# Rows sent to the experts without waiting for each other, and a later layer's keys and values made while they travel: a two-layer perceiver on one Trainium2 core

## The chip, the cores and the metric

The kernel runs on one core of a Trainium2 chip, all of it in float32. The metric is the device time of one execution in microseconds (us), lower is better. Engines are named as in the profile: PE is the matrix engine (TensorE) and PEld its weight loads, DVE the vector engine, ACT the scalar engine, POOL the GpSimd engine, SP the engine that issues most DMAs. "Cold" and "warm" stand for the half and the full TensorE clock that the profile's PEclk shows.

## The reference

A perceiver of two layers works on x of 16 × 64 rows of 256 (1024 rows in all) with a memory of 16 batches × 1601 rows. Each step adds to x what it makes of a layer norm of x:

```
x = x + L0_xattn(ln(x), memory)      # attention on the memory, 32 best scores of each row
x = x + L0_attn(ln(x))               # retention
x = x + L0_ffn(ln(x), ...)           # attention over 16 positions, then experts
x = x + L1_xattn(ln(x), memory)      # 16-head attention on the normed memory
x = x + L1_attn(ln(x))               # random features
x = x + L1_ffn(ln(x))                # fast feed-forward trees, then attention
```

The change lies in L0_ffn and in the start of L1_xattn:

```
y1 = _ln(x + _mha(x)) * ln1_g + ln1_b
# _moe: each row goes to its best of 8 experts, 128 rows for each expert
gates = softmax(y1 @ wg); idx = argmax(gates)
loc   = place of the row among those of the same expert
slot  = idx * cap + loc   if loc < cap else dropped
disp  = zeros.at[slot].set(y1)
h = disp @ w1 + b1 ;  y = h @ w2 + b2          # for each expert
out = gate_val * y[slot]                       # 0 for dropped rows
return _ln(y1 + out) * ln2_g + ln2_b
# L1_xattn, for each of the 16 batches:
qn, kn = layernorm(q), layernorm(memory)
Q, K, V = qn @ Wq + bq, kn @ Wk + bk, kn @ Wv + bv
```

## The kernel before, in words

All of x stands in the tile X, eight blocks of 128 rows (NB = 8, HALVES are blocks 0 to 3 and 4 to 7). A framework orders the instructions of each engine from the program's order, its data dependences, and the buffers of its pools; only the units of layer 1's attention (L1101 on) have an order written out by hand. A tile with a tag is one of a few buffers of its pool, so a new one waits until an older one is read.

The stages around the change:

- **Early memory.** Layer 1 needs for each of the 16 memory batches: the load (`load_mem`, L215 to L218, 1.6 MB into `memt`, two buffers), its normalisation (`normalise`, statistics on DVE at L415, the rows scaled on POOL at L426), its transposes (`turned_mem`, 26 transposes "pt" at L439 in eight groups, each copied by ACT at L444 into `mT`), its keys (`keys`, 8 tiles "ps_k" of two matmuls at L460, copied by ACT into kT at L468) and its values (`values`, 8 tiles "ps_v" at L482, copied into v at L490 or by ACT). For the first batches, 0 and 1, this is called early: fetches of 0 and 1, transposes, keys and values of batch 0, the fetch of batch 2, and the transposes of batch 1. In the program's text it stands behind L0_ffn, but the scheduler moves its instructions up into L0_ffn wherever PE would wait. Its PSUM pool `ps_early` has two buffers. A float32 matmul shows as two records, each a "pass" here.
- **MHA.** The transposes of xa = ln(X) (L165, "ps_t" in `transposed`), the projections of queries and keys ("ps_p", L183) and of values ("ps_n", L197), then four groups of two softmaxes: scores "ps_h" (L664), their mask and softmax on DVE (L672 to L684, the exponential on ACT), transposes "pt" (L688), "po" (L697), whose copies make oT; the output projection ("ps_n" again, L197), and `scaled`, which makes y1 by halves: moments on DVE (L141, L142), a square root on ACT (L144), its reciprocal (L145), and two DVE operations for each block.
- **Routing.** y1 is transposed, "ps_g" (L780) makes the gates, DVE picks the expert, "ps_c" (L810, L812) counts places, DVE makes `to_row` and `from_row`.
- **Scatter.** Eight indirect DMAs on POOL (L842) write the rows of y1 to the DRAM tensor `disp`, and one DMA on SP (L846) reads all of it into `dsp`:

```
for k in range(NB):
    nc.gpsimd.indirect_dma_start(out=disp, out_offset=...(ap=to_row[:, k : k + 1], axis=0),
        in_=y1[:, k, :], in_offset=None)
nc.sync.dma_start(out=dsp, in_=disp[0:NT, :].rearrange("(e p) d -> p e d", p=P))
```

  The framework sees eight writes to one tensor, at rows that it doesn't know.
- **Experts.** `dsp` is transposed (dT, L165), and for each of 8 experts "ps_h" (L859) and "ps_y" (L873, L876) follow, the copy `ye` on ACT (L878), and its store to `done`. The weights of an expert, 2 MB, come on SP through two buffers.
- **Gather.** Eight indirect DMAs on POOL (L883) fetch `back`, DVE adds each to y1 (L887), and when all are in the program, `scaled` norms y1 by halves into xa (L721) and `joined` (L892) adds each block to X.
- **Layer 1 begins.** qn is a norm of X (`layernorm`, L154 on DVE), transposed (L165) and copied by ACT (L944) into qnT, then projected: "ps_p" (L183), "ps_n" (L197). Then come the units.

At L1281 near the kernel's end, tree node scores are made with small matmuls, much as at L780.

Of the kernel before, what the change touches and what calls it, by code (L numbers as in the profile page):

```python
# [9 lines left out]
F32 = mybir.dt.float32  # L10
I32 = mybir.dt.int32
# [5 lines left out]
P = 128  # L17
# [48 lines left out]
def perceiver_kernel(  # L66
# [80 lines left out]

    HALVES = ((0, 4), (4, 4))

    def layernorm(dst, src, scale=1.0, bias=eps):  # L150
        for k0, n in HALVES:
            mv, rstd = moments(src, k0, n, scale, bias)
            for k in range(n):
                nc.vector.tensor_scalar(  # L154
                    dst[:, k0 + k, :], src[:, k0 + k, :], mv[:, k, 0:1], rstd[:, k : k + 1],
                    ALU.subtract, ALU.mult,
                )

    def transposed(src, pool, write):

        for half in range(2):
            for c in range(2):
                ps = pool.tile([P, 512], F32, name="ps_t", tag="mm")
                for j in range(4):
                    nc.tensor.transpose(  # L165
                        ps[:, j * P : (j + 1) * P],
                        src[:, half * 4 + j, c * P : (c + 1) * P],
                        ident,
                    )
                write(c, half, ps)  # L170
# [261 lines left out]
    def turned_mem(mt, mT, pool):  # L432

        for part, dc in TURN_STEPS:
# [12 lines left out]
            )  # L447
            yield

    def new_mT():  # L450
        return kvp.tile([P, 2, S], F32, name="mT", tag="mT")

    def keys(mT, kT, pool):

        for part, oc in KEY_STEPS:
            c0, _, n = PARTS[part]
            n0 = c0 * P
            ps = pool.tile([P, 512], F32, name="ps_k", tag="mm")
            for dc in range(2):
                nc.tensor.matmul(  # L460
                    ps[:, 0:n],
                    lhsT=wk[:, dc, oc * P : (oc + 1) * P],
                    rhs=mT[:, dc, n0 : n0 + n],
                    start=(dc == 0),
                    stop=(dc == 1),
                )
            yield
            nc.scalar.activation(  # L468
                kT[:, oc, n0 : n0 + n], ps[:, 0:n], AF.Identity, bias=col("L1_bk", oc)
            )  # L470
            yield

    def values(mT, v, pool, copy):

        c0 = 0
        for n in VALUE_STEPS:
            m = chunk(c0)
            ps = pool.tile([P, 2, D], F32, name="ps_v", tag="mm")
            for j in range(n):
                c = c0 + j  # L480
                for dc in range(2):
                    nc.tensor.matmul(  # L482
                        ps[0 : chunk(c), j, :],
                        lhsT=mT[:, dc, c * P : c * P + chunk(c)],
                        rhs=wv[:, dc, :],
                        start=(dc == 0),
                        stop=(dc == 1),
                    )
            yield
            copy(v[0:m, c0 : c0 + n, :], ps[0:m, 0:n, :])  # L490
            c0 += n
            yield
# [17 lines left out]
            pass  # L510

    kvs_of[0] = x1.enter_context(tc.tile_pool(name="x1_kv0", bufs=1))


    with ExitStack() as ph:
# [75 lines left out]
    with ExitStack() as ph:  # L591
# [21 lines left out]
        xa = keep.tile([P, NB, D], F32, name="xa")  # L613
        layernorm(xa, X)
        y1 = keep.tile([P, NB, D], F32, name="y1")

        with ExitStack() as sub:
            act = sub.enter_context(tc.tile_pool(name="mha_act", bufs=1))
# [94 lines left out]

            project(ps_m, w[:, 3, :, :], oT, add_mha)

        def scaled(dst, src, g, then):

            for k0, n in HALVES:
                mv, rstd = moments(src, k0, n)
                for k in range(n):  # L720
                    nc.vector.scalar_tensor_tensor(  # L721
                        dst[:, k0 + k, :], src[:, k0 + k, :], mv[:, k, 0:1], row(g),
                        ALU.subtract, ALU.mult,
                    )
                    then(k0 + k, rstd[:, k : k + 1])
# [4 lines left out]
            )  # L730

        scaled(y1, xa, "ln1_g", shifted)

        nc.gpsimd.tensor_tensor(
            X, X, row("ln2_b").unsqueeze(1).to_broadcast([P, NB, D]), ALU.add
# [2 lines left out]
        with ExitStack() as sub:  # L738
# [55 lines left out]
            nc.vector.reduce_sum(out=gs, in_=gates, axis=AX.X)  # L794
            nc.vector.reciprocal(gs, gs)
            nc.vector.tensor_tensor(gates, gates, gs.unsqueeze(2).to_broadcast(wide), ALU.mult)
            gval = act.tile([P, NB], F32, name="gval")
            nc.vector.reduce_max(out=gval, in_=gates, axis=AX.X)
            ranks = rank.unsqueeze(1).to_broadcast(wide)
            cand = act.tile(wide, F32, name="cand")  # L800
# [8 lines left out]
            ps = ps_x.tile([P, NB, NE], F32, name="ps_c", tag="mm")  # L809
            nc.tensor.matmul(ps, lhsT=before, rhs=mask, start=True, stop=False)  # L810
            for k in range(1, NB):
                nc.tensor.matmul(  # L812
                    ps[:, k:NB, :],
                    lhsT=ones,
                    rhs=mask[:, k - 1 : k, :].to_broadcast([P, NB - k, NE]),
                    start=False,
                    stop=(k == NB - 1),
                )
# [13 lines left out]
            to_row = act.tile([P, NB], I32, name="to_row")  # L832
            nc.vector.tensor_copy(to_row, slot)
            nc.vector.tensor_scalar(slot, slot, float(NT - 1), None, ALU.min)
            from_row = act.tile([P, NB], I32, name="from_row")
            nc.vector.tensor_copy(from_row, slot)
            nc.vector.tensor_tensor(gval, gval, fits, ALU.mult)


            dsp = act.tile([P, NE, D], F32, name="dsp", tag="y1T")  # L840
            for k in range(NB):
                nc.gpsimd.indirect_dma_start(  # L842
                    out=disp, out_offset=bass.IndirectOffsetOnAxis(ap=to_row[:, k : k + 1], axis=0),
                    in_=y1[:, k, :], in_offset=None,
                )
            nc.sync.dma_start(out=dsp, in_=disp[0:NT, :].rearrange("(e p) d -> p e d", p=P))  # L846
            dT = act.tile([P, 2, NT], F32, name="dT")
            transposed(dsp, ps_x, to_cols(dT))

            b1_at = COLS["moe_b1"][0]  # L850
            for e in range(NE):
                w1, w2, b2 = experts.pop(e) if e in experts else load_expert(e)
                hT = work.tile([P, 8, CAP], F32, name="hT", tag="hT")
                for g in range(2):
                    ps = ps_x.tile([P, 4, CAP], F32, name="ps_h", tag="mm")
                    for j in range(4):
                        f0 = (g * 4 + j) * P
                        for dc in range(2):
                            nc.tensor.matmul(  # L859
                                ps[:, j, :],  # L860
                                lhsT=w1[:, dc, f0 : f0 + P],
                                rhs=dT[:, dc, e * CAP : (e + 1) * CAP],
                                start=(dc == 0),
                                stop=(dc == 1),
                            )
                    at = b1_at + e * 8 + g * 4
                    nc.vector.tensor_tensor(
                        hT[:, g * 4 : (g + 1) * 4, :], ps,
                        cols[:, at : at + 4].unsqueeze(2).to_broadcast([P, 4, CAP]), ALU.add,
                    )  # L870
                ps = ps_x.tile([P, D], F32, name="ps_y", tag="mm")
                for f in range(8):
                    nc.tensor.matmul(  # L873
                        ps, lhsT=hT[:, f, :], rhs=w2[:, f, :], start=(f == 0), stop=False
                    )
                nc.tensor.matmul(ps, lhsT=ones[0:1, :], rhs=b2, start=False, stop=True)  # L876
                ye = work.tile([P, D], F32, name="ye", tag="ye")
                nc.scalar.copy(ye, ps)  # L878
                nc.scalar.dma_start(out=done[e * CAP : (e + 1) * CAP, :], in_=ye)

            for k in range(NB):
                back = work.tile([P, D], F32, name="back", tag="back", bufs=4)
                nc.gpsimd.indirect_dma_start(  # L883
                    out=back, out_offset=None, in_=done,
                    in_offset=bass.IndirectOffsetOnAxis(ap=from_row[:, k : k + 1], axis=0),
                )
                nc.vector.scalar_tensor_tensor(  # L887
                    y1[:, k, :], back, gval[:, k : k + 1], y1[:, k, :], ALU.mult, ALU.add
                )

        def joined(k, rstd):
            nc.vector.scalar_tensor_tensor(  # L892
                X[:, k, :], xa[:, k, :], rstd, X[:, k, :], ALU.mult, ALU.add
            )

        scaled(xa, y1, "ln2_g", joined)


    for b in range(2):
        run(fetch(b))  # L900
    for b in range(2):
        mTs[b] = new_mT()
        run(turned_mem(mems.pop(b), mTs[b], ps_early))
        if b == 0:
            kvs[0] = new_kv(0)
            mT = mTs.pop(0)
            run(keys(mT, kvs[0][0], ps_early))
            run(values(mT, kvs[0][1], ps_early, nc.scalar.copy))
            run(fetch(2))
    early.close()  # L910

    with x1 as ph:
# [23 lines left out]


        qn = act.tile([P, NB, D], F32, name="qn", tag="b")
        layernorm(qn, X, 1.0 + EPS, eps2)
        qnT = act.tile([P, 2, NT], F32, name="qnT", tag="a")  # L940

        def normed(dst, wname, bname):
# [552 lines left out]
```

## Time and profile before

| | us |
|---|---|
| median of 3 runs | 1711.45 (1711.29 to 1711.51) |
| the profiled execution | 1709.81 |
| its span, first to last instruction | 1708.1 |
| PE busy in it | 1512.6 (89%) |
| DVE busy | 1021.2 (60%) |
| ACT busy | 814.6 (48%) |
| POOL busy | 212.0 (12%) |
| mean granted TensorE clock | 0.954 |

The times in the views are of this one execution. In the row of slices the span is cut into 40 equal parts and each digit is a busy share in tenths. A row of a windows table gives the stretch, then the busy time of each engine with the number of instructions, then the granted clock and what the DMA engines did. A row of the timeline gives the start, the busy time, engine, line, operation, output and inputs, and in brackets the idle time ahead of it with what ended it. A row of the chain of waits gives a start, a length, and the engine and operation that the end of the kernel was waiting for.

### The profile page before, as it was taken

To read this page: it belongs to the slowest core of one execution; us is meant where nothing else is said; L and a number is where in the kernel's file an instruction comes from. 1 tells how busy PE (TensorE), PEld (TensorE's weight loads), DVE (VectorE), ACT (ScalarE), POOL (GpSimd) and SP (SyncE) were. 2 spreads that over 40 slices of the span, in tenths; PEclk is the share of its full clock that TensorE was granted. 3 is DMA by queue.
4 is the path that set the end of the run, shared out by engine and by line. 5 is a ranking of instruction groups with operands and counts; after the bars stand their busy time and mean duration, and the time that the engine had idled before them with its cause. 6 is when DMAs were issued, how large, how long until landed. Compare 5 with 4: busy or idle time off the path is not lost.

```text
span 1708.1 us, 27877 instructions
## 1 busy us (share of the span) xinstructions
PE 1512.6 (89%) x10992; PEld 1008.2 (59%) x10992; DVE 1021.2 (60%) x2197; ACT 814.6 (48%) x1984; POOL 212.0 (12%) x405
## 2 busy tenths in 40 slices
PE   4899979992939999999999999999999973889997
PEld 3555546672836666666666666666667652544455
DVE  2667847771145777677767776777766665333122
ACT  3455531350005766666667666766666551212121
POOL 0000004201010120222021202120210001000000
PEclk9999989995969999999999999999999996889999
DMA  9044203223910101110011101110100003100000
GB/s 316 1 154 138 94 19 108 83 91 97 287 58 1 40 3 41 40 41 15 29 40 41 34 11 41 40 41 3 41 2 3 3 3 122 66 1 0 0 0 25
DMA packets 76034, 92.84 MB, mean 54 GB/s; under 512 B 2408, under 2 KB 71072, under 8 KB 75776
## 3 DMA queue, kind: packets, MB, share of 16 engines
q1 hardware_dynamic: 72064, 80.85, 14.9%
q0 software_dynamic: 2688, 9.17, 1.9%
q8 instruction: 86, 1.41, 0.4%
q10 hardware_dynamic: 1152, 1.05, 0.2%
q14 instruction: 44, 0.36, 0.1%
HBM read 85.82 MB, written 5.24 MB: 53 GB/s over the span
## 4 chain that ended last, share of the span: by engine, by line
PE 72%; ACT 10%; DVE 9%; issue 4%; DMA 3%; SPq 1%; POOL 0%; ACTq 0%; DVEq 0%; POOLq 0%
PE ps_v L482 10%; PE ps_k L460 7%; ACT a L997 6%; PE sc L981 6%; PE po L1029 6%; PE pt L1010 5%; PE ps_h L1334 5%; PE ps_p L183 3%; PE ps_o L1352 3%; PE pt L248 3%; PE sc L290 3%; PE pu L346 3%; PE pt L439 2%; PE ps_n L197 2%; DVE nmax L995 2%
## 5 line engine op out<-in xcount | busy, mean ns | idle before, releaser
L997 ACT ACTIVATE a<-sc,nmax 128x384 f32<-128x384 f32 (+2 forms) x512 | 300.3, 596 | 170.8 <-DVE nmax L995 170.5
L995 DVE TENSOR_REDUCE nmax<-sc 128x1 f32<-128x384 f32 (+2 forms) x512 | 258.2, 567 | 109.8 <-PE sc L981 109.7
L482 PE MATMUL ps_v<-w_x,mT 128*128 128x256 f32 (+1 forms) x832 | 205.3, 385 | 22.3 <-ACT kT L468 22.3
L1010 PEld LDWEIGHTS pt<-ident,a 128*128 128x128 f32 (+1 forms) x1664 | 189.3, 141 | 52.1 <-issue 28.2
L1017 DVE COPY aT<-pt 128x512 f32<-128x512 f32 (+1 forms) x288 | 191.0, 685 | 37.8 <-PE pt L1010 30.8
L1010 PE MATMUL pt<-ident,a 128*128 128x128 f32 (+1 forms) x1664 | 207.5, 274 | 2.3 <-ACT kT L468 0.7
L460 PE MATMUL ps_k<-mT,w_x 128*128 128x384 f32 (+2 forms) x512 | 207.9, 528 | 0.1
L482 PEld LDWEIGHTS ps_v<-w_x,mT 128*128 128x128 f32 (+1 forms) x832 | 144.7, 186 | 49.6 <-ACT kT L468 31.3
L460 PEld LDWEIGHTS ps_k<-mT,w_x 128*128 128x128 f32 x512 | 87.4, 190 | 108.1 <-issue 77.6
L1029 PE MATMUL po<-aT,v 128*32 128x128 f32 (+1 forms) x3328 | 119.1, 277 | 10.9 <-DVE aT L1017 7.0
L444 ACT ACTIVATE mT<-pt,cols 128x384 f32<-128x384 f32 (+2 forms) x128 | 87.1, 684 | 79.0 <-PE pt L439 76.3
L981 PE MATMUL sc<-kT,qh 32*128 32x384 f32 (+2 forms) x1024 | 123.1, 548 | 0.0
L426 POOL TENSOR_SCALAR memt<-memt,m_nmean,m_rstd 128x256 f32<-128x256 f32 (+1 forms) x208 | 112.2, 557 | 7.3 <-PE po L1029 4.3
L997 ACT ACTIVATION_READ_ACCUMULATOR a<-sc,nmax 128x1 f32 x512 | 105.1, 205 | 0.0
L1029 PEld LDWEIGHTS po<-aT,v 128*32 128x32 f32 (+1 forms) x3328 | 82.7, 109 | 35.5 <-issue 13.5
L490 DVE COPY v<-ps_v 128x512 f32<-128x512 f32 (+1 forms) x120 | 69.2, 576 | 49.3 <-PE po L1029 30.7
L415 DVE BATCH_NORM_STATS2 m_st<-memt 128x6 f32<-128x256 f32 (+1 forms) x208 | 82.6, 401 | 3.4 <-DMA memt<-in_mem_dram 3.0
L1334 PE MATMUL ps_h<-xnT,fw 128*128 128x512 f32 x192 | 84.1, 596 | 0.0
L253 ACT COPY mT<-pt 128x512 f32<-128x512 f32 (+1 forms) x128 | 58.0, 503 | 53.3 <-PE pt L248 52.6
L248 PE MATMUL pt<-ident,memt 128*128 128x128 f32 (+1 forms) x416 | 63.2, 292 | 22.8 <-DMA memt<-in_mem_dram 21.6
L468 ACT ACTIVATE kT<-ps_k,cols 128x384 f32<-128x384 f32 (+2 forms) x128 | 76.0, 593 | 13.2 <-PE ps_k L460 13.2
L1015 ACT COPY aT<-pt 128x512 f32<-128x512 f32 x128 | 76.9, 601 | 0.7 <-PE pt L1010 0.7
(310 smaller groups left out, 1945.8 us busy)
## 6 DMA issues: line engine op xcount, KB each, us to landing
memt<-in_mem_dram SPq DMA_DIRECT2D x32, 1536.0 KB, 9.1
w<-in_moe_w_dram SPq DMA_DIRECT2D x16, 1024.0 KB, 5.1
fw<-in_fff_w_dram SPq DMA_DIRECT2D x6, 1024.0 KB, 12.8
memt<-in_mem_dram SPq DMA_DIRECT2D x32, 65.0 KB
w_x<-in_w_x_dram POOLq DMA_DIRECT2D x2, 1024.0 KB, 12.2
rows<-in_rows_dram POOLq DMA_DIRECT2D x1, 1430.5 KB, 9.9
X<-in_x_dram SPq DMA_DIRECT2D x1, 1024.0 KB
w_mha<-in_w_mha_dram POOLq DMA_DIRECT2D x1, 1024.0 KB
```

The lines of the kernel that those rows point to most:

```text
L248: nc.tensor.transpose(pt[:, j * P : j * P + chunk(c)], mems[h][0 : chunk(c), c, dc * P : (dc + 1) * P], ident[0 : chunk(c), 0 : chunk(c)],)
L426: nc.gpsimd.tensor_scalar(mt[0:m, c, :], mt[0:m, c, :], nmean[0:m, c : c + 1], rstd[0:m, c : c + 1], ALU.add, ALU.mult,)
L444: nc.scalar.activation(mT[:, dc, c0 * P : c0 * P + n], pt[:, 0:n], AF.Identity, bias=col("L1_norm_b", dc), scale=col("L1_norm_w", dc),)
L460: nc.tensor.matmul(ps[:, 0:n], lhsT=wk[:, dc, oc * P : (oc + 1) * P], rhs=mT[:, dc, n0 : n0 + n], start=(dc == 0), stop=(dc == 1),)
L482: nc.tensor.matmul(ps[0 : chunk(c), j, :], lhsT=mT[:, dc, c * P : c * P + chunk(c)], rhs=wv[:, dc, :], start=(dc == 0), stop=(dc == 1),)
L981: nc.tensor.matmul(scs[j][:, 0:n], lhsT=qh[rs, oc, b, :, :], rhs=kT[rs, oc, c0 * P : c0 * P + n], start=True, stop=True,)
L995: nc.vector.reduce_max(out=nm, in_=sc[:, 0:n], axis=AX.X, negate=True)
L997: nc.scalar.activation(aj[:, 0:n], sc[:, 0:n], AF.Exp, bias=nm, accum_out=tot[:, blk, part : part + 1])
L1010: nc.tensor.transpose(pt[0:m, j * P : (j + 1) * P], a[j][:, c * P : c * P + m], ident)
L1017: nc.vector.tensor_copy(aT[0:m, :], pt[0:m, :])
L1029: nc.tensor.matmul(po[32 * j : 32 * j + 32, :], lhsT=v[0:m, c0 + c, blk * 32 : (blk + 1) * 32], rhs=aTs[c][0:m, j * P : (j + 1) * P], star ...
L1334: nc.tensor.matmul(ps, lhsT=fw1[:, f, dc, m * P : (m + 1) * P], rhs=xnT[:, dc, cs], start=(dc == 0), stop=(dc == 1),)
```

## The change

Scatters: the eight indirect writes are declared independent of each other, and the read of `disp` gets a dependence on each of the eight by hand. Gathers: each half is fetched, added, normed and joined to X before the second half is fetched in the program's text. Early memory: the transposes of batch 0 are called after y1; its keys are held behind the last "ps_c" matmul and dT's transposes behind its last key matmul; its values are held behind the last expert's last matmul; the transposes of batch 1 and the fetch of batch 2 are called after that. The norm qn is called by halves, the first at high priority, and in it every second block is made by ACT (Identity, with scale and a bias `ln_off` that DVE makes) instead of DVE. The tiles `gval` and `from_row` move to a pool that lives longer.

```diff
-    def layernorm(dst, src, scale=1.0, bias=eps):
-        for k0, n in HALVES:
+    def layernorm(dst, src, scale=1.0, bias=eps, halves=HALVES, shared=False):
+        for k0, n in halves:
             mv, rstd = moments(src, k0, n, scale, bias)
+            if shared:
+                off = small.tile([P, NB], F32, name="ln_off", tag="ln_off")
+                nc.vector.scalar_tensor_tensor(
+                    off[:, 0:n], mv[:, 0:n, 0], -1.0, rstd[:, 0:n], ALU.mult, ALU.mult
+                )
             for k in range(n):
+                if shared and k % 2:
+                    nc.scalar.activation(
+                        dst[:, k0 + k, :], src[:, k0 + k, :], AF.Identity,
+                        bias=off[:, k : k + 1], scale=rstd[:, k : k + 1],
+                    )
+                    continue
...
+    def early_memory(b):
+        run(fetch(b))
+        mTs[b] = new_mT()
+        run(turned_mem(mems.pop(b), mTs[b], ps_early))
...
         scaled(y1, xa, "ln1_g", shifted)
+        early_memory(0)
...
             dsp = act.tile([P, NE, D], F32, name="dsp", tag="y1T")
+            sent = []
             for k in range(NB):
-                nc.gpsimd.indirect_dma_start(
+                sent.append(nc.gpsimd.indirect_dma_start(
                     out=disp, out_offset=bass.IndirectOffsetOnAxis(ap=to_row[:, k : k + 1], axis=0),
                     in_=y1[:, k, :], in_offset=None,
-                )
-            nc.sync.dma_start(out=dsp, in_=disp[0:NT, :].rearrange("(e p) d -> p e d", p=P))
+                ).ins)
+                for other in sent[:-1]:
+                    tc.declare_no_dep(sent[-1], other, reason="rows of disp")
+            read = nc.sync.dma_start(
+                out=dsp, in_=disp[0:NT, :].rearrange("(e p) d -> p e d", p=P)
+            ).ins
+            for one in sent:
+                tc.add_manual_dep(
+                    read, one.name,
+                    mybir.DependencyInfo(mybir.DependencyClass.Sync, mybir.DependencyReason.DATA),
+                    reason="rows of disp",
+                )
+            mT0 = mTs[0]
+            kvs[0] = new_kv(0)
+            with tc.issue_after(counted.ins):
+                run(keys(mT0, kvs[0][0], ps_early))
             dT = act.tile([P, 2, NT], F32, name="dT")
-            transposed(dsp, ps_x, to_cols(dT))
+            with tc.issue_after(made[-1].ins):
+                transposed(dsp, ps_x, to_cols(dT))
...
+            with tc.issue_after(last.ins):
+                run(values(mTs.pop(0), kvs[0][1], ps_early, nc.scalar.copy))
+            def joined(k, rstd):
                 nc.vector.scalar_tensor_tensor(
-                    y1[:, k, :], back, gval[:, k : k + 1], y1[:, k, :], ALU.mult, ALU.add
-                )
...
+                    X[:, k, :], xa[:, k, :], rstd, X[:, k, :], ALU.mult, ALU.add
+                )
+            for half in HALVES:
+                for k in range(half[0], half[0] + half[1]):
+                    back = work.tile([P, D], F32, name="back", tag="back", bufs=4)
+                    nc.gpsimd.indirect_dma_start(
...
+                    nc.vector.scalar_tensor_tensor(
+                        y1[:, k, :], back, gval[:, k : k + 1], y1[:, k, :], ALU.mult, ALU.add
+                    )
+                scaled(xa, y1, "ln2_g", joined, (half,))
-    for b in range(2):
-        run(fetch(b))
-    for b in range(2):
-        mTs[b] = new_mT()
-        run(turned_mem(mems.pop(b), mTs[b], ps_early))
-        if b == 0:
-            kvs[0] = new_kv(0)
-            mT = mTs.pop(0)
-            run(keys(mT, kvs[0][0], ps_early))
-            run(values(mT, kvs[0][1], ps_early, nc.scalar.copy))
-            run(fetch(2))
+    early_memory(1)
+    run(fetch(2))
...
-        layernorm(qn, X, 1.0 + EPS, eps2)
+        with tc.high_priority():
+            layernorm(qn, X, 1.0 + EPS, eps2, HALVES[0:1], True)
+        layernorm(qn, X, 1.0 + EPS, eps2, HALVES[1:2], True)
```

What the change moves in the instruction order of each engine: on PE, batch 0's keys leave MHA for the place between "ps_c" and dT's transposes, its values leave MHA and the output projection for the place behind the last "ps_y", and batch 1's transposes follow them; batch 0's transposes stay before MHA. On SP, the load of batch 2 goes behind the last expert's weights. On ACT, behind the last `ye`, stand copies of values, the square root of y's first half, more copies of values, batch 1's eight copies, then the square root of y's second half and that of X's first. On DVE, the first half's joins and qn's first half precede the second half's joins. Up to 298 us and behind 533 us of the execution before, the order is as it was.

## The prediction

> **What bounds the kernel now.** I read the page's slices and its chain by engine first, then the windows cut at the stages that the diff touches, then the timeline of POOL and of PE inside those windows.
>
> ```profile
> PE   4899979992939999999999999999999973889997
> PE 72%; ACT 10%; DVE 9%; issue 4%; DMA 3%; SPq 1%; POOL 0%; ACTq 0%; DVEq 0%; POOLq 0%
> ```
>
> PE carries the kernel. One slice is 42.7 us; slices 10 (384 to 427 us) and 12 (470 to 512 us) have PE at 2 and 3 tenths. Those are the two spans in which rows travel to the experts and back.
>
> ```profile
> core 0: us, PE busy (x) PEld busy (x) DVE busy (x) ACT busy (x) POOL busy (x), PEclk, DMA share, GB/s
> 323.00:335.00 12.00, 11.36 (x79) 9.48 (x78) 9.04 (x18) 1.26 (x2) 1.20 (x3) 0.92 0.01 1
> 335.00:352.00 17.00, 17.00 (x90) 10.77 (x90) 13.83 (x28) 7.73 (x14) 0.00 (x0) 0.95 0.00 0
> 352.00:365.00 13.00, 13.00 (x84) 10.06 (x82) 8.88 (x18) 6.29 (x12) 0.00 (x0) 1.00 0.01 2
> 391.40:418.20 26.80, 0.00 (x0) 0.00 (x0) 0.11 (x1) 0.00 (x0) 7.90 (x8) 0.50 0.24 78
> 418.20:484.60 66.40, 66.29 (x416) 58.06 (x416) 12.45 (x18) 3.78 (x9) 0.00 (x0) 0.97 0.65 204
> 484.60:512.20 27.60, 0.00 (x0) 0.01 (x1) 17.75 (x68) 2.55 (x5) 8.47 (x9) 0.54 0.15 43
> ```
>
> 327 to 365 us is layer 0's MHA: PE is full, but DVE is busy 0.68 to 0.81 of the time too, so PE is full because keys and values fill it. The two gaps of 26.8 and 27.6 us have no matmul at all; the experts between are PE-bound.
>
> ```profile
> 391.39 1.14 POOL L842 DMA_INDIRECT disp<-y,to_row  x1 [17.79 <-DVE slot L834]
> 394.25 1.00 POOL L842 DMA_INDIRECT disp<-y,to_row  x1 [1.72 <-DMA disp<-y,to_row]
> 410.30 0.96 POOL L842 DMA_INDIRECT disp<-y,to_row  x1 [1.71 <-DMA disp<-y,to_row]
> 412.86 0.37 SPq L846 DMA_DIRECT2D dsp<-disp  x1
> 488.92 0.97 POOL L883 DMA_INDIRECT back<-done,from_row  x1 [0.30 <-issue]
> 490.19 0.95 POOL L883 DMA_INDIRECT back<-done,from_row  x1 [0.30 <-issue]
> ```
>
> Each scatter waits for the one before to land: eight at 2.70 us, the brackets name a DMA as the releaser. The gathers, which have no such wait, start every 1.26 us.
>
> ```profile
> 331.00:332.00 1.00, 0.53 (x5) 0.34 (x4) 1.00 (x2) 0.59 (x1) 0.00 (x0) 1.00 0.00 0
> 332.00:333.00 1.00, 0.83 (x7) 0.83 (x8) 1.00 (x3) 0.25 (x1) 0.00 (x0) 1.00 0.00 0
> 333.00:334.00 1.00, 1.00 (x4) 0.63 (x4) 1.00 (x3) 0.38 (x1) 0.00 (x0) 0.58 0.00 0
> 422.00:423.00 1.00, 1.00 (x11) 1.00 (x11) 0.65 (x1) 0.00 (x0) 0.00 (x0) 1.00 0.00 0
> 418.27 3.65 PE L165 MATMUL ps_t<-ident,dsp 128*128 128x128 f32 x16 [28.70 <-DMA dsp<-disp]
> 379.50 3.46 PE ps_g L780 x30
> 1486.15 5.62 PE L1281 MATMUL ps_t<-nodes,xnT 128*128 128x45 f32 x26
> ```
>
> These carry the clock, which decides much here. At 333.2 us it falls to half although PE was not idle, only 0.53 and 0.83 busy in the two microseconds before. It comes back at 421.9 us, after 16 dense transposes that took 3.65 us at half speed. A small pass costs 0.115 us warm (3.46/30) and 0.21 us cold (5.41 us of the 26 passes of L1281 lie on the chain).
>
> **The change, part by part** (us against before; minus is a gain; each with its range).
>
> 1. *Before MHA.* Three key tiles sat among the transposes of xa (12 passes, 4.4 us, partly in waits for xa). They leave; the projections start when the last transpose is evicted: −0.75 (0 to −1). Mem 0's transposes stay where they were.
>
> 2. *MHA, 327.05 to 365.05.* On the chain of waits some 9.7 us of keys and 11.4 us of values lie here, 21 us of 38. This is not a gain of 21: what they covered is DVE's. A group of two softmaxes costs DVE 2 × (0.69 + 0.60 + 0.60 + 0.60 + 0.09 + 0.60) = 6.4 us, four groups 25.5, and the chain through exp (0.6), four transposes (0.44), their eviction (0.6), po (1.02) and its eviction (0.6) is not all covered. I replayed the new order with in-order queues and the rows' durations: 36.5 us at full clock, a gain of 1.5. But without the fill PE is busy about half the time, and the 331 to 334 us rows say that this drops the clock. With transposes at 0.88 and po at about 2 to 2.6 per group, a group's period goes from 7.0 to 8.4 us, and the stage to about 41.5: **+3.5** (−1.5 to +5).
>
> 3. *Output projection and y1.* The last values leave L197's stretch, but it begins cold: a block takes 1.72 instead of 0.86 for two or three blocks, until the dense run raises the clock: +2 (0 to +2.5). From there to y1 DVE is the bound (12.7 us), unchanged. The 32 gate passes (30 recorded) go from 0.115 to 0.21 each if cold: +2.8 (0 to +3.3). In exchange mem 1's eight transposes and ACT evictions go; they stood beside DVE's work: 0. The ACT queue is shorter, which I count as 0.
>
> 4. *Scatters.* Without their mutual wait POOL issues each in about 1.0 plus 0.3, as the gathers do: pitch 1.27. The last starts at 391.4 + 7 × 1.27 = 400.3, 400.4 as the first issue took 0.14 longer, and lands 2.4 later, 402.8, where before it landed at 412.72: **−9.9** (−8 to −10.1). The new semaphore waits are on SP's read: eight in place of one, nothing queued behind it but the weights of expert 2, whose buffers are still in use. The read takes its 5.3 us and lands at 408.2.
>
> 5. *Keys in this gap.* 32 passes of mean 0.41 (six of them took 2.49 from 300.80 on; the page's mean of 528 ns is over the shapes and clocks of the whole run) start when ps_c ends at 389.6, about 13 us warm, plus 2.3 for a cold beginning, and two PSUM buffers emptied by ACT (0.59 each, idle here): done near 405. The transposes of dT are put behind them, but their data comes at 408.2. Cost 0, cover 3 us; if that were gone, it costs what keys overrun. They find PE warm: 1.83 in place of 3.65 for 16, **−1.3** taken (0 to −1.8; three idle microseconds lie between).
>
> 6. *Experts:* 66.4, PE-bound, same matmuls: 0. The load of the third batch (SP, before at 379 us) now sits behind the last expert weights and waits for mem 1's transposes at about 504; it is first used at 555 us: 0.
>
> 7. *Second gap.* Before, DVE's last join of a half, its statistics and norms set the end: sqrt of the first half at 496.3, qn's first half at 511.72, its second at 515.02. Now PE has 52 value passes from 484.6, copied by ACT, then mem 1's 26 transposes with eight ACT evictions of about 0.65; PE ends near 504, nothing else needs it before qn. ACT's queue is new: half 1's square root stands between value copies, half 2's (wanted at 504.8) behind the eight evictions ending at 504.2: a margin of 0.6 us. On DVE the order turns: X's first half joined, its statistics and qn first. DVE sheds four norms (4 × 0.34, now 0.4 to 0.78 on ACT) and gets two small ops (2 × 0.17). First half of qn about 506.8 instead of 511.7 to 513.1, second at 512.9 instead of 516.4. The trace shows no Identity at 128×256 here; the nearest, ye's copy of that shape, is 0.37, the 512-wide one 0.78. Then eight cold transposes (1.1 per four) and four projections: the end moves from 526.1 to about 523.3: **−2.8** (−1.5 to −4.5, the former if ACT is late by a microsecond).
>
> Sum: −0.75 + 3.5 + 2 + 2.8 − 9.9 − 1.3 − 2.8 = **−6.5**. The profiled execution took 1709.81 us (span 1708.1 and 1.7 around it), 1.6 under the median of 1711.45; a difference carries over, so the forecast is 1711.45 − 6.5 = 1704.9.
>
> **Where a rule would change the sum.** The Trainium skill, "TensorE: Matmul & The Clock Gate", section "HAM oscillation — how this bites in real kernels", gives the gate's rule as a PE idle gap longer than about 3.4 us. By it MHA would stay warm: no gap of that length arises between its groups, and steps 2 and 3 would be −1.5, 0 and 0, the sum −16.75 with −1.8 in step 5. The row of 333.2 us differs: half clock after a stretch with no such gap, only a PE partly busy. I follow the row; the rule is the rival below. It speaks against the change in the other direction too: taking fill out of a partly idle PE is what cools it.
>
> **The rivals.**
> - *The clock stays up* (the rule taken literally): −0.75 − 1.5 − 9.9 − 1.8 − 2.8 = −16.75, 1694.7. For it: transposes alone raised it at 421.9, and PE stays about half busy. Against: the fall at 333.2. Chance 0.15.
> - *The gaps' gain is paid back in MHA:* steps at their upper ends, +5 + 2.5 + 3.3 against −0.75 − 9.5 − 0 − 1.5: −1, that is 1710.5, no change. For it: PE stood in for nothing there, DVE is near full. Chance 0.17.
> - *The scatters stay serial* (slower): the declaration takes only the semaphore away, and POOL or its queue still processes one at a time. Each 0.1 us of pitch over 1.27 costs 0.7; at 2.2 the sum is zero, at 2.70, as now, it is +3.4: 1714.8. The same if SP's read is not released by the last landing. For it: 128 rows of 1 KB in each; against: gathers of the same size run at 1.26. This, with keys overrunning 408 us, 0.08.
>
> **How the numbers follow.** The forecast's own chance is 0.60, with 1701 to 1709. This kernel's measurement tells about 0.2%, 3.4 us: faster is below 1708.0, slower above 1714.9. The forecast gives nearly all of its 0.60 to faster, the warm case 0.15, a part of the payback case falls below 1708: 0.75 together; 0.18 stays within; slower 0.07. The range leaves out the warmest and the slowest cases: 1695.5 to 1710.5.
>
> **What would show it.** Right: scatters at a pitch near 1.27 with the last started at about 400 (shifted by what came before); keys between ps_c and dT, ending before dsp lands; PEclk near 0.5 in MHA and its span 40 to 42 us; 30 gate passes in about 6.3 us; 16 dT transposes in about 1.9; qn's halves apart by 5 us and the unit stage 2 to 4 us sooner than the experts' end says. Wrong: MHA at PEclk 1.0; a scatter bracket that still ends in "DMA"; dT waiting for PE rather than for dsp; a square root at 505 to 508 us waiting behind mem 1's evictions, with DVE idle before L145.

## The result and the profile after

Nine executions of the changed kernel have a median of 1703.4 us (1702.03 to 1708.67), nine of the kernel before 1711.29 (1709.27 to 1712.99): a ratio of 0.996, 95% interval 0.9948 to 0.9972, or 7.9 us less. The forecast was 1704.9, 6.5 less. Seven of the nine lie between 1702.0 and 1703.7 and two at 1708.5 and 1708.7. The first profile is of one of the two (1708.67), a second (e1 below) of an execution of 1702.07 us. Both are read here. Of the 6.6 us between them 2.0 lie ahead of all that was changed: the second reaches xa's first transpose at 298.12, the first at 300.13, with the same order of work up to there (before: 299.11). The rest is mainly where the clock fell.

The page's slices for PE in the first profile:

```profile
PE   4899979867989999999999999999999973889997
```

and the windows of the same stretches as before:

```profile
335.00:352.00 17.00, 12.20 (x58) 9.03 (x60) 14.24 (x28) 4.28 (x7) 0.00 (x0) 0.51 0.00 0
352.00:365.00 13.00, 7.21 (x39) 5.00 (x36) 10.34 (x21) 3.74 (x7) 0.00 (x0) 0.50 0.00 0
391.40:418.20 26.80, 17.92 (x54) 11.77 (x54) 3.99 (x22) 5.02 (x9) 7.88 (x8) 0.75 0.24 78
484.60:512.20 27.60, 20.41 (x91) 15.24 (x89) 17.72 (x70) 14.19 (x25) 8.50 (x9) 0.83 0.34 102
```

The two thin slices, 10 and 12 (2 and 3 tenths), are now 7 and 8; instead, slices 8 and 9, in which MHA lies, have gone from 9 and 9 to 8 and 6. Both gaps hold matmuls, and in MHA PE is busy 0.72 and 0.55 of the two stretches, at a PEclk of 0.50. Its DVE (14.24 of 17 us) is about as busy as before, 13.83.

POOL's timeline with SP's read behind it, first profile:

```profile
401.09 1.13 POOL L866 DMA_INDIRECT disp<-y,to_row  x1 [21.75 <-DVE slot L856]
402.52 0.99 POOL L866 DMA_INDIRECT disp<-y,to_row  x1 [0.30 <-issue]
410.14 0.96 POOL L866 DMA_INDIRECT disp<-y,to_row  x1 [0.31 <-issue]
412.83 0.37 SPq L872 DMA_DIRECT2D dsp<-disp  x1
```

The brackets no longer name a DMA, and the pitch is (410.14 − 401.09) / 7 = 1.29 us. But the first scatter starts 9.7 us later than before (391.39), so the read is issued at 412.83, where before it was at 412.86: in this execution the projections, MHA, y1 and the gates had spent the whole gain before it was made.

PE's timeline of the first profile:

```profile
303.79 1.57 PE L177 MATMUL ps_t<-ident,xa 128*128 128x128 f32 x8 [1.97 <-DVE xa L166]
306.28 16.59 PE L195 MATMUL ps_p<-xaT,w_mha 128*128 128x512 f32 x32 [0.92 <-ACT xaT L132]
386.25 6.41 PE L803 MATMUL ps_g<-wg,y1T 128*128 128x8 f32 x30
418.36 3.65 PE L177 MATMUL ps_t<-ident,dsp 128*128 128x128 f32 x16 [5.98 <-DMA dsp<-disp]
```

and of the second:

```profile
301.80 1.31 PE L177 MATMUL ps_t<-ident,xa 128*128 128x128 f32 x8 [1.99 <-DVE xa L166]
304.13 14.00 PE L195 MATMUL ps_p<-xaT,w_mha 128*128 128x512 f32 x32 [1.01 <-ACT xaT L132]
381.72 6.41 PE L803 MATMUL ps_g<-wg,y1T 128*128 128x8 f32 x30
413.85 3.65 PE L177 MATMUL ps_t<-ident,dsp 128*128 128x128 f32 x16 [5.36 <-DMA dsp<-disp]
```

Where the three key tiles used to stand, PE now waits two microseconds for the second half of xa. In the second execution no fall of the clock follows; in the first it fell after the same wait (1.97 against 1.99 us), and 32 passes took 16.59 instead of 14.00 us. The gates are cold in both, and dT's transposes find PE cold in both, after more than five idle microseconds.

The stages, read from PE's, POOL's and SP's timelines of the profiled execution of each kernel (names of the runs are those of the next section). A stage starts where the one before it ends: y1 with its last transpose, the gates, dT and the experts with the end of their last pass or copy, the others with the first instruction of the next stage. Between the gates and the first scatter 8.4 us of routing, alike in all columns, are left out.

| us | before | after, 1st | after, 2nd | e2 | e5 | e7 | e12 | e4 | e6 |
|---|---|---|---|---|---|---|---|---|---|
| projections for MHA | 21.02 | 23.61 | 21.02 | 21.02 | 21.02 | 21.02 | 21.01 | 21.03 | 21.02 |
| MHA, scores to output projection | 37.84 | 39.48 | 39.16 | 37.84 | 37.69 | 35.13 | 36.02 | 36.19 | 37.88 |
| to the last transpose of y1 | 14.61 | 17.09 | 17.62 | 14.62 | 14.64 | 15.52 | 14.62 | 14.61 | 14.61 |
| gates' matmuls | 3.46 | 6.20 | 6.20 | 3.45 | 6.45 | 6.21 | 3.45 | 3.45 | 3.45 |
| first scatter to the read | 21.47 | 11.74 | 11.75 | 11.82 | 11.76 | 11.75 | 11.83 | 11.81 | 11.81 |
| read to dT | 5.41 | 5.53 | 5.53 | 5.96 | 5.55 | 5.37 | 6.16 | 6.09 | 6.15 |
| dT's transposes | 3.65 | 3.65 | 3.65 | 3.65 | 3.65 | 3.59 | 3.65 | 3.64 | 1.94 |
| experts | 62.64 | 63.67 | 62.65 | 63.71 | 62.82 | 62.59 | 63.59 | 63.41 | 62.58 |
| second gap, to the units | 48.37 | 45.90 | 44.76 | 47.29 | 44.92 | 44.79 | 43.58 | 43.43 | 43.27 |

### The profile page after: what moved, and what is told of

It is laid out like the page before. It is cut to its first block, busy times and chain, and to the rows that moved or that the text cites. A ratio compares the mean times of both kernels' runs of the same rounds, so it can differ in the third digit from the quotient of the medians.

```text
span 1706.8 us, 27883 instructions
## 1 busy us (share of the span) xinstructions
PE 1537.3 (90%) x10992; PEld 1024.3 (60%) x10992; DVE 1020.3 (60%) x2195; ACT 818.1 (48%) x1988; POOL 210.9 (12%) x405
## 3 DMA queue, kind: packets, MB, share of 16 engines
q1 hardware_dynamic: 72064, 80.85, 14.6%
## 4 chain that ended last, share of the span: by engine, by line
PE 51%; ACT 9%; DVE 6%; issue 3%; DMA 1%; POOL 0%; ACTq 0%; DVEq 0%; SPq 0%; POOLq 0%
PE ps_v L497 9%; ACT a L1034 7%; PE sc L1018 6%; PE ps_k L475 6%; PE po L1066 6%; PE pt L1047 5%; PE ps_h L1371 5%; PE ps_o L1389 3%; PE pt L451 2%; DVE nmax L1032 2%; PE ps_v L1402 2%; ACT kT L483 1%; ACT aT L1052 1%; DVE m_st L427 1%; PE pt L1099 1%
```

## The experiments

All were compared with the kernel before on the same chip; its medians were 1709.67 (e1 to e4), 1710.71 (e5 to e8), 1709.79 (e9 to e11) and 1710.05 us (e12).

**e1: the changed kernel again**, no edit.

> The changed kernel once more, unedited, for a second profile: the first profiled execution took 1708.67 us where the median of nine was 1703.4. Theory (the clock's phase): where a span with PE half idle falls against the clock's steps differs from execution to execution, so an execution near 1703 has the full clock in stretches where the first profile has half: the projections of MHA (L195) in 14.0 instead of 16.6 us, and MHA starting near 327.5 instead of 329.9, or the first expert at full clock from its start. Rival: the 5 us lie behind 533 us, in layer 1, and everything up to the experts stands as in the first profile (gates' last pass ending 9.7 us later than before).

Four executions, median 1702.74, ratio 0.9956 (0.9941 to 0.9971). The profiled one has the projections at 14.00 us and MHA starting at 325.15; behind the first unit the two profiles are alike (1175.2 and 1175.3 us to the end). The rival falls. The clock's place accounts for the projections (2.6 us), and in the experts and the second gap the first profile is 1.0 and 1.1 longer; the 2.0 us ahead of xa's transposes are not explained. In the execution of 1702 us, against before: MHA +1.3, y1 +3.0, gates +2.7, scatters −9.7, second gap −3.6, together −6.3. Another 1.9 lie ahead of the projections: 0.9 of them step 1 of the forecast, and 1.0 ahead of the first changed instruction, so not the change's.

**e2: the scatters alone**, in the kernel before.

```diff
+                for other in sent[:-1]:
+                    tc.declare_no_dep(sent[-1], other, reason="rows of disp")
...
+                tc.add_manual_dep(
```

> The kernel before with the scatters declared independent and nothing else; keys and values stay in MHA, the gather and qn as before. Theory: the gap shrinks by 9.8 us and nothing gives it back, 1711.3 - 9.8 = 1701.5, faster than the whole change (1703.4); the scatters at a pitch of 1.27 us. Rival (the gap alone is not worth what it measures: the expert weights or the read of the dispatched rows become the bound): 1705 to 1711.

Median 1699.87, ratio 0.9939 (0.9925 to 0.9952): 9.8 us, as expected. The interval overlaps that of the whole change (0.9948 to 0.9972) at its edge, but each of its five executions (1698.49 to 1701.20) is shorter than each of the thirteen of the changed kernel (from 1702.03 on). The scatters alone give more than the whole change, and the rest of it gives some 3 us back.

**e3: the changed kernel with the scatters serial**, the counterpart: the eight declarations taken out again.

> The changed kernel with the scatters waiting for each other again; everything else as changed. Theory (keys and values taken out of MHA cost 2 to 7 us through the clock, the later halves win 2.5): 1703.4 + 9.8 = 1713.2, no faster than before. Rival (the moves are worth something of their own, the scatters not all): 1706 to 1709.

Median 1714.14 of 16 executions, ratio 1.0024 (1.0016 to 1.0031): slower than before. POOL's timeline is the old one (`[1.70 <-DMA disp<-y,to_row]`, pitch 2.69). So the moves and the halves together cost about 4.5 us without the scatters.

**e4: the fill left where it was**: the changed kernel with keys, values, batch 1's transposes and the fetch of batch 2 as in the kernel before.

```diff
-        early_memory(0)
...
-            with tc.issue_after(counted.ins):
-                run(keys(mT0, kvs[0][0], ps_early))
...
-            with tc.issue_after(last.ins):
-                run(values(mTs.pop(0), kvs[0][1], ps_early, nc.scalar.copy))
...
-    early_memory(1)
-    run(fetch(2))
+    for b in range(2):
+        run(fetch(b))
+    for b in range(2):
+        mTs[b] = new_mT()
+        run(turned_mem(mems.pop(b), mTs[b], ps_early))
+        if b == 0:
...
+            run(keys(mT, kvs[0][0], ps_early))
+            run(values(mT, kvs[0][1], ps_early, nc.scalar.copy))
+            run(fetch(2))
```

> The changed kernel with batch 0's keys and values, batch 1's transposes and the fetch of batch 2 where the kernel before has them (in MHA and around y1); scatters independent, gather and join by halves, qn by halves with every second block on ACT. Theory: MHA keeps its full clock, and both gaps keep their gains: 1711.3 - 9.8 - 2.8 = 1698.7, some 5 us under the changed kernel; MHA in 38.0 us and gates' passes at 0.115 us. Rival (the fill delays MHA's own passes as much as the low clock does): 1702 to 1704, as the changed kernel.

Median 1695.12, ratio 0.9922 (0.9908 to 0.9935): 14.6 us under before, lower than the 1698.7 expected, and 7.6 under the changed kernel's 1702.74; two of its five executions took 1698.7 and 1699.2. The gates take 3.45 us, y1 14.61. The moves of keys, values and transposes are thus a loss of about 7 us inside a change that wins 8.

**e5: fill without purpose.** In the changed kernel the 84 passes of batch 0's keys and values are made twice, once for nobody: 68 of them in MHA, 12 ahead of the projections (where the three key tiles had stood), the last four behind it.

```diff
         early_memory(0)
+        warm(mTs[0])
```

> The changed kernel plus the fill without its purpose: in MHA, exactly where the kernel before has batch 0's keys and values, the same 84 matmul passes are made a second time, into PSUM tiles that nobody reads; the real ones stay in the gaps. It adds 21 us of PE work and takes none away. Theory (the loss in MHA, y1 and the gates is the half clock that follows from a thinly used PE): PEclk back to 0.9 or more from 335 to 390 us, the gates' 30 passes in 3.5 instead of 6.2 us, the stretch from the output projection to y1's last transpose in 14.6 instead of 17 us, total 1702.7 - 2.7 - 2.7 - 1 = 1696 to 1697. Rival (the loss comes from the order and from what else moved, not from the clock): no better than the changed kernel, 1702.7 to 1706.

(`warm` makes the matmuls of `keys` and `values` into `ps_early`, without the copies.) Median 1699.52, ratio 0.9933 (0.992 to 0.9947): PE is busy 22 us more in MHA, 28 in all, and 3 to 4 us are won, fewer than the theory's 6 to 7. Windows of the second profile of the changed kernel, and of this run:

```profile
337.00:347.00 10.00, 6.58 (x38) 4.58 (x38) 8.01 (x16) 2.44 (x4) 0.00 (x0) 0.67 0.00 0
347.00:357.00 10.00, 5.92 (x36) 4.20 (x32) 7.87 (x16) 2.83 (x6) 0.00 (x0) 0.55 0.00 0
377.00:387.00 10.00, 7.54 (x38) 7.27 (x38) 5.20 (x15) 2.75 (x4) 0.00 (x0) 0.65 1.02 381
```

```profile
337.00:347.00 10.00, 10.00 (x51) 6.07 (x50) 7.14 (x15) 2.41 (x5) 0.00 (x0) 0.94 0.00 0
347.00:357.00 10.00, 10.00 (x58) 7.42 (x57) 9.66 (x19) 2.87 (x5) 0.00 (x0) 1.00 0.01 2
377.00:387.00 10.00, 8.33 (x40) 7.68 (x40) 4.09 (x10) 2.17 (x3) 0.00 (x0) 0.61 0.96 359
```

The clock of MHA is back (0.55 to 1.00) and y1's stage with it (17.62 to 14.64). But in the last window it is still at 0.61, and the gates take 6.45 us: half of the theory is right. What else had stood there before are batch 1's transposes.

**e6: busy gaps**: e4 with 19 and 23 unread 128×512 matmuls in the two gaps.

```diff
+            with tc.issue_after(counted.ins):
+                warm(19)
...
+            with tc.issue_after(last.ins):
+                warm(23)
```

> The fastest kernel so far (fill left in MHA, 1695.1), with 19 matmuls of 128x512 that nobody reads behind the last place count, and 23 behind the last expert, so that PE is busy in both gaps. Theory: the 16 transposes of the dispatched rows take 1.8 instead of 3.65 us, the expert starts warm, and qn's transposes and first projections run at full clock: -1.8 and about -1.5, 1691.8. Rival (the clock falls in the last idle microseconds before the rows land in spite of it, or the matmuls stand in front of qn): 1695 to 1697.

Median 1694.2, ratio 0.9906 (0.9891 to 0.9921), where 1691.8 was expected; the interval overlaps e4's. PE's timeline in this run:

```profile
410.31 1.94 PE L177 MATMUL ps_t<-ident,dsp 128*128 128x128 f32 x16 [0.75 <-DMA dsp<-disp]
```

That is the gain expected of dT (1.7 us), but the second gap is shorter than e4's by no more than 0.2. The two medians are 0.9 us apart, which these runs don't tell from nothing. This execution's MHA took 37.88 us, e4's 36.19, with the same instructions: here the clock fell for 3.4 us from 334.2 on, early in MHA, and in e4 it did not. The same fall stands in the profiles of before, e2 and e8 (333.2, 332.3 and 333.1; 37.84, 37.84 and 37.85 us), which have this fill too. So 1.7 us of MHA are a matter of the execution, and an MHA with this fall is compared only with others that have it.

**e7: keys back in MHA**, values still in the second gap.

```diff
         early_memory(0)
+        kvs[0] = new_kv(0)
+        run(keys(mTs[0], kvs[0][0], ps_early))
...
-            with tc.issue_after(counted.ins):
-                run(keys(mT0, kvs[0][0], ps_early))
```

> The changed kernel with batch 0's keys back in MHA (they fill its first half) and only the values in the second gap, with batch 1's transposes behind them. Theory (the clock needs fill for as long as MHA lasts): it falls in MHA's second half instead of its first, so output projection, y1's transposes and gates are still cold: 1700.5 to 1702. Rival (half of the fill is enough to keep the clock up to the gates): 1695 to 1697.

Median 1699.68, ratio 0.9936 (0.9922 to 0.9949), a little better than the 1700.5 to 1702 expected. MHA is the shortest of all, 35.13 us, y1 15.52, but the gates still 6.21. Fill is not free: without the early fall of the clock MHA takes 35.13 us with keys alone and 36.19 with keys and values (e4), even though in e7 the clock is down for seven microseconds from 352 on; with the early fall it is 36.83 (e10, below) and 37.84.

**e8: all of qn on DVE**, in e4: `layernorm(...)` by halves without the last argument.

> As the fastest kernel so far (fill left in MHA, 1695.1), but all of qn made on DVE as before; the halves of gather, join and qn stay. Theory (the halves carry the second gap's gain, ACT's share is small: two norms of 0.34 us less on DVE for each half, less the extra small operation of 0.17): 1695.1 + 0.5 to 1.0 = 1695.6 to 1696.1. Rival (the share on ACT carries it): 1697 to 1699.

Median 1696.36, ratio 0.9915 (0.9901 to 0.9928), near the theory and not to be told from e4's. In the profiles the second gap is 43.97 against 43.43; the halves carry the gain (47.29 in e2), ACT's share some 0.5 us.

**e9: batch 1's transposes put back around y1**, keys and values in the gaps.

```diff
+        run(fetch(1))
...
+            with tc.issue_after(outed.ins):
+                mTs[1] = new_mT()
+                run(turned_mem(mems.pop(1), mTs[1], ps_early))
...
-    early_memory(1)
```

> The changed kernel with one move undone: batch 1's 26 transposes stand around y1's transposes again, behind the output projection, as in the kernel before; keys and values of batch 0 stay in the gaps. Theory (it is these transposes whose leaving let the clock fall before the gates, since the kernel with MHA filled but without them still had gates of 6.4 us): gates' 30 passes back to 3.5 us though MHA is still cold, and the eight copies of ACT gone from the second gap: 1702.7 - 2.7 - 0.5 to 1 = 1699.0 to 1699.5. Rival (the gates are cold because MHA was): gates 6.2 us, 1701.5 to 1703.

(`outed` is the output projection's last matmul.) Median 1702.92, ratio 0.9962 (0.9949 to 0.9976): nothing won. In the profile the gates take 5.10 us, the clock falling at 384.9 in the middle of them, and the second gap is 43.27; from the projections to the units it is 1.9 us shorter than the changed kernel's second profile, but 1.4 longer behind them, which is not explained. Alone, this move is not shown to help.

**e10 and e11: mixtures** for the shortest time: keys in MHA, batch 1's transposes around y1, values in the first gap; e11 with 6 and 23 unread matmuls in what is left of the gaps.

> A mixture for the shortest time: keys in MHA (its first half, as in the run with keys put back), batch 1's transposes around y1 as in the kernel before, values in the first gap behind the last place count, nothing in the second gap; scatters independent, halves and ACT's share as changed. Theory: MHA in 35 to 36 us, the gates warm at 3.5 us, the second gap in 43.4 us as in the kernel with the fill left: 1694 to 1695, at or just below that kernel's 1695.1. Rival (MHA's cold second half makes the output projection and y1 a microsecond or two longer): 1696 to 1697.

> The mixture with matmuls that nobody reads in what is left of the gaps: 6 of 128x512 behind the values, 23 behind the last expert. Theory: the transposes of the dispatched rows at 1.9 in place of 3.65 us, the experts' first microsecond warm: 2 to 2.5 us under the mixture without them, 1692 to 1693. Rival (as the other kernel with busy gaps showed, only 1 us of it arrives): 1693.5 to 1694.

Medians 1697.74 and 1696.78, ratios 0.9923 (0.9909 to 0.9936) and 0.9925 (0.9911 to 0.9939): no better than e4, and they miss their expectations by 3 and 4 us. In their profiles MHA takes 36.8 us, in spite of keys alone, and the gates 4.6 to 4.7, the clock falling in the middle of them; in e11 dT takes 1.97. MHA's 36.8 against e7's 35.13 are the early fall again (334.9 and 334.5 us, for 3.4 us): 1.7 us, as between e6 and e4.

**e12: e5 and e9 together.**

> The changed kernel with both stand-ins together: the 84 passes that nobody reads in MHA, and batch 1's transposes around y1's; batch 0's real keys and values stay in the gaps. PE's order from MHA to the gates is then that of the kernel before, with 21 us of work added. Theory (PE's density, through the clock, is the whole of the loss): output projection to y1's last transpose 14.6 us, gates 3.5 us, MHA 36.2 to 37.8, second gap 43.3: 1702.8 - 1.5 - 3.0 - 2.7 - 1.5 = about 1694, level with the kernel with the fill left (1695.1), in spite of the added work. Rival (with the transposes alone put back, nothing was won in the total, so something else stands against it): 1698 to 1700.

Median 1695.91, ratio 0.992 (0.9906 to 0.9934): with 26 us of useless PE work in it, some 7 us faster than the changed kernel and level with e4, though not the 1694 expected. Its windows:

```profile
337.00:347.00 10.00, 10.00 (x54) 5.99 (x53) 8.73 (x18) 3.03 (x5) 0.00 (x0) 1.00 0.00 0
347.00:357.00 10.00, 10.00 (x68) 7.92 (x66) 9.63 (x20) 2.87 (x5) 0.00 (x0) 1.00 0.01 2
367.00:377.00 10.00, 9.26 (x57) 7.16 (x56) 10.00 (x35) 4.77 (x10) 0.97 (x4) 1.00 0.45 151
```

and its gates in PE's timeline (3.45 us of it behind y1's last transpose):

```profile
378.20 3.52 PE L836 MATMUL ps_g<-wg,y1T 128*128 128x8 f32 x30
```

The real keys and values are in the gaps here too, so it is not where they stand that costs, but what PE's clock does without something in their place. With MHA filled, batch 1's transposes take the gates from 6.45 (e5) to 3.45 us. In the medians both fills are needed: either alone gives 1699.5 (e5) and 1702.9 (e9), both 1695.9. Whether the gates themselves need MHA filled is not shown: in e9 they start warm and the clock falls 2.0 us into them, in e12 it falls only 1.3 us behind them.

## Why the prediction was right, and where not

The forecast of 6.5 us less met 7.9 (6.9 in e1) by the mechanism it named: scatters win ten, MHA and what follows pay most of it back through the clock, the halves win a few. In the execution of 1702 us the stages of its own steps sum to −7.0. That this is within 0.5 of the forecast is in part luck: step 2 was 2.2 us too dear and step 7 0.8, steps 3 and 5 were 0.9 and 1.3 too cheap, and these cancel. Step by step, on that execution:

- *Step 1*, −0.75: the first transpose of xa to the projections went from 6.92 to 6.01 us, −0.9. What the step did not see is that the tiles' place becomes a two-microsecond wait, after which the clock may fall: +2.6 in the first profile.
- *Step 2*, +3.5: +1.3 (+1.6 in the first profile; the span is 39.2 and 39.5 us, under the 40 to 42 named as a sign). PE is cold as forecast, and its passes are if anything longer than the replay had them (first profile: four transposes 1.09 to 1.12 us, po 0.69 + 1.97). But PE still waits 1.9 to 2.7 us for DVE once in each group, so less of them lay on the path: a group's period was put at 8.4 us and is 7.7 (from po's start at 343.66 to 366.72, three periods), of which DVE is busy some 6.4. (By the step's own figures, four groups at 1.4 more would have been 42.1, not 41.5.) And the +1.3 is against an MHA with the early fall; against e4's, without it, the step is +3.0.
- *Step 3*, +2 and +2.8: +3.0, above its range, and +2.7. The sum is near, one term's cause is not: batch 1's transposes were costed at nothing, "they stood beside DVE's work". e5, with MHA filled, still had gates of 6.45 us; with the transposes as well (e12) they were at 3.45.
- *Step 4*, −9.9: −9.7, and e2 shows that it stands alone.
- *Step 5*: keys done 5.4 to 6 us before the rows land, in place of 3, so at no cost; but the −1.3 for warm transposes of dT was wrong, 3.65 in both. The clock fell again in the idle stretch ahead of them, at 417.3 and 410.7 us. With that stretch filled (e6), they take 1.94.
- *Step 6*, 0: 62.65 and 62.64; in the first profile +1.0, where the clock rose one step later.
- *Step 7*, −2.8: −3.6. The square root behind batch 1's copies, the danger named, cost nothing: it stands 19.8 us behind the last expert with and without them (e1, e4). In e4 the gap is 1.3 us shorter still. The two differ in the order of qn's second transposes (e4 starts the projection after two of the eight, the changed kernel after all), but that is not the reason: e8 has the changed kernel's order and takes 16.40 us from the first of these transposes to the end of the projections, e4 16.50, the second profile 17.88. What differs is when the clock comes back: 3.0 and 3.4 us after that transpose in e8 and e4, 6.0 in the second profile (at 507.2, 505.9 and 513.1 us). The old code shows the same difference: 17.51 us before, with the clock back after 5.4, and 16.39 in e2, after 3.1. PE's timeline in the second profile of the changed kernel, and then in e8:

```profile
507.10 2.13 PE L177 MATMUL ps_t<-ident,qn 128*128 128x128 f32 x8 [4.29 <-DVE qn L166]
509.03 9.05 PE L195 MATMUL ps_p<-qnT,w_x 128*128 128x512 f32 x16
```

```profile
504.23 2.18 PE L177 MATMUL ps_t<-ident,qn 128*128 128x128 f32 x8 [3.81 <-DVE qn L166]
506.21 7.51 PE L195 MATMUL ps_p<-qnT,w_x 128*128 128x512 f32 x16
```

Of the rivals, the warm clock is excluded by the rows of MHA (0.50 to 0.67), the serial scatters by POOL's brackets. The payback did not come in the size it named (10.8 us in MHA, y1 and the gates): the two profiles pay 7.1 and 6.9 there. The two executions near its 1710.5 (1708.5 and 1708.7) owe that to other stages, as far as the one of them that was profiled shows. The rule of the Trainium skill that was weighed ("TensorE: Matmul & The Clock Gate", "HAM oscillation — how this bites in real kernels": gaps of about 3.4 us) would have given 1694.7; in this case the clock fell after a wait of 1.97 us, and following the row gave the better forecast. The reason read from that row, a thin PE, is only half of it: the last section has the same busy share without a fall.

What stays open: what beside PE's busy share decides a fall; where the two microseconds between the two profiles ahead of 300 us come from; and e9's total.

The shortest times are e4's and e6's (0.9922 and 0.9906), and e8, e10, e11 and e12 are not to be told from e4 either; e4 makes no unread matmuls, and is the one to keep.

## What to carry to other kernels

Before work is moved out of a stage into an idle gap, ask what the stage does without it: the chain of waits through MHA alternates between DVE's softmax and the PE passes that stayed (second profile), so taking some 22 us of PE work out won nothing there, and with PE's work so thin its clock fell to 0.55 to 0.67 (second profile), in y1's stage and the gates too. Idle PE time in a gap costs only what the path through the gap costs, and shortening that path (a wait that needn't be, a join by halves) was worth all of the gain. A change of several parts should be run in parts: one of these alone beat the whole.

## What the runs showed of the hardware

The clock's steps lie on a fixed grid. In the first profile PEclk changed, among other places, at 304.7, 311.5, 335.4, 417.3 and 424.2 us, in the second at 332.2, 342.4 and 345.8. The last two are 3.41 apart, and the first profile's differences, 6.8, 23.9, 81.9 and 6.9, are 2, 7, 24 and 2 times that; the clock records of all fourteen profiles fit the same spacing, each at its own offset against the program. One and the same two-microsecond wait was followed by a fall in one execution and not in the other:

```profile
304.00:305.00 1.00, 1.00 (x8) 0.70 (x6) 1.00 (x4) 0.00 (x0) 0.30 (x1) 0.85 1.06 360
305.00:306.00 1.00, 0.36 (x2) 0.00 (x0) 0.89 (x2) 0.81 (x1) 1.00 (x1) 0.50 1.10 388
```

```profile
302.00:303.00 1.00, 1.00 (x8) 0.60 (x6) 1.00 (x4) 0.00 (x0) 0.29 (x1) 1.00 1.08 369
303.00:304.00 1.00, 0.12 (x2) 0.00 (x0) 1.00 (x2) 0.96 (x1) 1.00 (x1) 1.00 1.07 365
```

First profile above, second below: the same instructions, PEclk 0.50 and 1.00. Counted back in steps of 3.41, the first profile's wait (301.8 to 303.8) lies whole between two steps, 301.3 and 304.7, and the second's (299.8 to 301.8) is cut by one at 301.5. That this decides is not tested, and PE's busy share between two steps does not decide alone. Before, and then e4, each between two steps in the first microseconds of MHA:

```profile
329.75:333.16 3.41, 2.77 (x25) 2.41 (x21) 3.41 (x6) 1.04 (x2) 0.00 (x0) 1.00 0.00 0
331.80:335.21 3.41, 2.77 (x18) 2.06 (x17) 3.41 (x6) 1.25 (x2) 0.00 (x0) 1.00 0.00 0
```

PE is busy 2.77 of 3.41 us in both. The clock fell at the end of the first, at 333.2, and stayed up behind the second. The first stretch holds only scores (L664), the second some of the key passes too; whether that is the difference is open. A fall there cost 1.7 us of MHA in each of three pairs of profiles (e6 and e4, e5 and e12, e10 and e7). So one profile of each kernel is not enough to say what an edit costs, to a microsecond or two.
